# Four-layer conv_seq kernel: the token-major copy of layer 1's x made by vector-engine squares and DRAM transfers instead of TensorE transposes

## The chip, the core and the metric

The kernel is one program on one core of a Trainium2 chip, all arithmetic in float32. The metric is the device time of one execution in microseconds; the median of three runs before the change is 2450.09 us (2449.71 to 2451.28). The engines are TensorE (PE, with its weight loads shown apart as PEld), the vector engine (DVE), the scalar engine (ACT), GpSimd (POOL), and SyncE (SP), which issues every DMA of this kernel.

## The reference

x has four batches, 512 channels and 32x32 positions, that is 1024 tokens. Four layers follow each other:

- Layer 0: attention with 8 heads of 64 over the tokens, output projection, residual.
- Layer 1: linear attention, the subject of the change. With xf of shape (b, c, n):

```
Q = einsum('bcn,mc->bmn', xf, wq) + bq        # m = 64
K = einsum('bcn,mc->bmn', xf, wk) + bk
V = einsum('bcn,oc->bon', xf, wv) + bv
V = (max(xf, -1) + mean(xf, -1)) * V
Qf, Kf = softplus(Q)^T, softplus(K)
KV = einsum('bmn,bcn->bmc', Kf, V)
norm = 1 / einsum('bnm,bm->bn', Qf, sum(Kf, -1) + EPS)
x = x + gamma * einsum('bnm,bmc,bn->bcn', Qf, KV, norm)
```

- Layer 2: layer norm over the channels, attention with one head of 512, projection, residual.
- Layer 3: group norm, attention with 4 heads of 128, projection, residual.

## The kernel before

x of a batch lies in SBUF as 128 partitions x 4 chunks of channels x 1024 tokens; batches not in use go home to DRAM and come back. Most large products are made in seven half-size products instead of eight (`seven_products`, p1 to p7), whose sums and joins run on DVE (L774, L780, L739) and whose weight sums run on POOL (L695 to L698).

The kernel computes layer 1 without ever forming V: K^T x is formed first (`keys_times_x`, tokens on the contraction axis) and multiplied by wv afterwards (`keys_times_values`). For K^T x both the keys and x must have tokens on partitions. The function `linear_attention` returns seventeen pieces for one batch. They are: `gates` (the maximum over tokens on DVE, L1414, the sums on ACT, L1417); two `features` products of queries and keys, after which ACT adds a bias (L1407) and `softplus` runs over DVE and ACT (L1385 to L1391, with scratch tiles e, u and l); four `transpose_x`, each eight 128x128 transposes on TensorE (L1425) into PSUM and a copy of 128x1024 to a scratch tile, by ACT (L1432) or DVE (L1430) in turn; `transpose_keys` (L1438), which reads the block that the softplus wrote; `keys_times_x` (L1454), two calls to a piece; then the sum of keys, the division of queries, the transpose of K^T x, the product with wv (wv1, loaded at L599), and two `update` pieces.

Layer 1 of batch b-1 is woven into layer 0's projection of batch b: after every second product `slot()` emits one piece. This happens for batches 0, 1 and 2 (near 220, 460 and 700 us). Batch 3 has its pieces between the products of layer 2's start (950 to 1040 us), beside a layer norm. PE's program is in the order in which the code emits it; the other engines' programs are ordered by a scheduler, and every engine executes its program in order. So a piece that waits on PE holds everything behind it.

The scratch tiles are the v tiles of the batch being projected (batches 0 to 2) or a rotation of four tiles (batch 3). e is scratch 0, u scratch 1, l scratch 2; the ACT copies of `gates` go to scratch 3. x transposed, xt i, goes to scratch (i + 3) mod 4. The tile family "many" has one buffer; before the change it holds sums of probabilities in the attentions.

Lines that matter besides: L1084 and L1092 are layer 0's output projection of the same batch and its additions to x, L1051 the normalisation of the attention's output by quotients that come by DMA (L1033), L686 to L689 the four sums of a projection's inputs, L947 and L950 the sums of probabilities, L1492 a copy of the divided queries to the other 64 partitions.

## Time and profile before

| | |
|---|---|
| median of 3 runs | 2450.09 us (2449.71 to 2451.28) |
| profiled execution, its own time | 2450.76 us |
| its span, first to last instruction | 2449.0 us |
| PE busy | 2433.3 us |
| DVE busy | 1506.1 us |
| ACT busy | 704.6 us |
| POOL busy | 251.1 us |
| data moved by DMA | 88.64 MB, 36 GB/s on the mean |
| transposes of x on PE | 128, between 251.2 and 1003.2 us |

The time exceeds the span by 1.8 us, which lies around the program. The profile's times are counted from the start of the span. A line of a timeline gives start, duration, engine, source line, operation, output and inputs, shape and count, and in brackets the idle time of the engine ahead of it and what ended it. Durations of matmuls overlap, so PE's cost of a group is the distance to the next start. An "idle before" on PE itself would be time lost; on the other engines it is slack.

### The profile page before, as it was taken

The numbers are of one execution on the slowest core, as the hardware profiler recorded it, in microseconds if no ns is written. First come the engines' busy times: TensorE is split into PE (matmuls) and PEld (weight loads), VectorE is DVE, ScalarE is ACT, GpSimd is POOL, SyncE is SP. The second block draws the span as 40 slices with busy tenths as digits, with TensorE's granted clock in tenths as the row PEclk, the third lists the DMA queues.
The fourth block names the chain that finished last, engine by engine and source line by source line (L and its number), as shares of the span: only waits on it lengthen the run. The fifth ranks groups of instructions, "written<-read, shape, count | busy, mean of one in ns | idle before, by whom it ended". The sixth has DMA issues, their size and how long they took to land.

```text
span 2449.0 us, 24662 instructions
## 1 busy us (share of the span) xinstructions
PE 2433.3 (99%) x10098; PEld 1225.7 (50%) x10098; DVE 1506.1 (61%) x1798; ACT 704.6 (29%) x864; POOL 251.1 (10%) x240
## 2 busy tenths in 40 slices
PE   9999999999999999999999999999999999999999
PEld 4544544453455344644645446445556456555653
DVE  3677577757775788656595774763554554445344
ACT  1454144415531653221211201112321430332132
POOL 4001100110010001101103021021010001002000
PEclk9999999999999999999999999999999999999999
DMA  5000020002000301011001010110010001001001
GB/s 185 7 12 18 5 78 10 18 5 79 19 9 13 130 23 48 5 69 39 31 1 69 5 74 13 52 69 18 35 69 1 18 35 52 1 35 35 1 22 45
DMA packets 28959, 88.64 MB, mean 36 GB/s; under 512 B 2508, under 2 KB 10188, under 8 KB 25895
## 3 DMA queue, kind: packets, MB, share of 16 engines
q1 hardware_dynamic: 28838, 87.00, 9.9%
q8 instruction: 81, 1.33, 0.2%
q14 instruction: 40, 0.32, 0.0%
HBM read 60.59 MB, written 25.35 MB: 35 GB/s over the span
## 4 chain that ended last, share of the span: by engine, by line
PE 99%; DVE 1%; ACT 0%; issue 0%; DMA 0%; SPq 0%; DVEq 0%
PE acc L707 20%; PE acc L832 12%; PE acc L967 9%; PE acc L982 9%; PE sc L936 9%; PE sc L931 9%; PE acc L839 8%; PE acc L1084 7%; PE acc L1316 6%; PE acc L1277 2%; PE feat L641 1%; PE acc L1018 1%; PE acc L641 1%; PE upd L1520 1%; PE acc L1454 1%; PE xt L1425 1%
## 5 line engine op out<-in xcount | busy, mean ns | idle before, releaser
L941 ACT ACTIVATE pt<-sc 128x1024 f32<-128x1024 f32 x384 | 379.2, 1022 | 541.2 <-PE sc L936 304.0
L950 DVE TENSOR_TENSOR sum<-sum,pt 128x1024 f32<-128x1024 f32 x256 | 314.6, 1229 | 159.0 <-ACT pt L941 146.5
L967 PE MATMUL acc<-pt,v 64*64 64x512 f32 x2048 | 247.6, 591 | 0.0
L931 PE MATMUL sc<-q,k 64*64 64x512 f32 x2048 | 245.0, 591 | 1.1 <-ACT pt L941 1.1
L982 PE MATMUL acc<-pt,v 128*128 128x512 f32 x512 | 240.8, 594 | 0.0
L936 PE MATMUL sc<-q,k 128*128 128x512 f32 x512 | 239.9, 594 | 0.0
L707 PE MATMUL acc<-t,ws 128*128 128x512 f32 x384 | 173.9, 594 | 0.0
L695 POOL TENSOR_TENSOR ws<-wqkv 128x256 f32<-128x256 f32 (+1 forms) x40 | 39.7, 992 | 1307.1 <-PE acc L1018 523.2
L947 DVE TENSOR_TENSOR sum<-pt 128x1024 f32<-128x1024 f32 x64 | 78.0, 1219 | 137.4 <-ACT pt L941 137.4
L982 PEld LDWEIGHTS acc<-pt,v 128*128 128x128 f32 x512 | 96.8, 190 | 125.1 <-issue 121.4
L936 PEld LDWEIGHTS sc<-q,k 128*128 128x128 f32 x512 | 97.1, 191 | 115.9 <-issue 92.7
L967 PEld LDWEIGHTS acc<-pt,v 64*64 64x64 f32 x2048 | 78.3, 133 | 142.5 <-issue 140.3
L931 PEld LDWEIGHTS sc<-q,k 64*64 64x64 f32 x2048 | 77.3, 133 | 140.9 <-issue 131.9
L707 PEld LDWEIGHTS acc<-t,ws 128*128 128x128 f32 x384 | 72.6, 190 | 86.5 <-issue 85.0
L746 ACT COPY v<-acc 128x512 f32<-128x512 f32 x24 | 14.0, 585 | 308.6 <-PE acc L832 308.6
L678 DVE RECIPROCAL rd<-acc 128x512 f32<-128x512 f32 (+1 forms) x24 | 80.5, 3353 | 29.1 <-PE acc L1018 29.1
L832 PE MATMUL acc<-ws,t 128*128 128x256 f32 x384 | 87.3, 380 | 0.0
L839 PE MATMUL acc<-qs,w 128*128 128x512 f32 x192 | 86.6, 593 | 0.0
L839 PE MATMUL acc<-q,ln 128*128 128x512 f32 x192 | 85.8, 593 | 0.0
L1084 PE MATMUL acc<-ot,wo 128*128 128x256 f32 x336 | 80.7, 383 | 2.7 <-ACT ou L1103 2.7
L737 DVE TENSOR_TENSOR v<-acc,v 128x512 f32<-128x512 f32 x72 | 49.5, 689 | 51.5 <-PE acc L832 51.2
L746 ACT COPY q<-acc 128x512 f32<-128x512 f32 x40 | 23.4, 585 | 197.1 <-PE acc L707 197.1
(326 smaller groups left out, 3476.0 us busy)
## 6 DMA issues: line engine op xcount, KB each, us to landing
home<-x SPq DMA_DIRECT2D x8, 2048.0 KB
x<-home SPq DMA_DIRECT2D x8, 2048.0 KB
out<-x SPq DMA_DIRECT2D x32, 256.0 KB
rds<-quotients SPq DMA_DIRECT2D x30, 256.0 KB
rds<-quotients SPq DMA_DIRECT2D x7, 1024.0 KB
x<-in_x SPq DMA_DIRECT2D x3, 2048.0 KB
wo<-in_wo SPq DMA_DIRECT2D x3, 1024.0 KB
w<-in_w SPq DMA_DIRECT2D x1, 3072.0 KB
```

The source lines that it names most:

```text
L678: nc.vector.reciprocal(rd, ps)
L707: nc.tensor.matmul(ps, lhsT=w[:, m, :], rhs=x[:, m, :], start=start, stop=stop, skip_group_check=True)
L832: nc.tensor.matmul(ps[:, bass.ts(r, C // 2)], lhsT=x[:, m, bass.ts(2 * o + r, P)], rhs=w[:, m, :], start=(start and r == 0), stop=stop, sk ...
L839: nc.tensor.matmul(ps, lhsT=x[:, m, bass.ts(o, P)], rhs=w[:, m, :], start=start, stop=stop, skip_group_check=True,)
L931: nc.tensor.matmul(ps[half(h), s, :], lhsT=key(g, i)[half(s), half(h)], rhs=q[qb][half(s), g, :], start=True, stop=True,)
L936: nc.tensor.matmul(ps[:, s, :], lhsT=key(g, 2 * i + s), rhs=q[qb][:, g, :], start=True, stop=True)
L941: exps.append(nc.scalar.activation(pt, ps, AF.Exp, scale=scale).ins)
L950: adds.append(nc.vector.tensor_tensor(acc, acc, pt, ALU.add).ins)
L967: nc.tensor.matmul(outs[qb, g][r][half(s), :], lhsT=v[i // 2][half(r), i % 2, g * P + s * hd : g * P + (s + 1) * hd], rhs=pt[half(r), s, : ...
L982: nc.tensor.matmul(outs[qb, g][0], lhsT=v[j // 2][:, j % 2, bass.ts(g, P)], rhs=pt[:, s, :], start=(j == 0), stop=(j == NT - 1),)
L1084: nc.tensor.matmul(ps[i][:, bass.ts(o, n)], lhsT=w[:, m, bass.ts(o, P)], rhs=t[:, m, :], start=(start and m + o == 0), stop=(stop and m == ...
L1316: nc.tensor.matmul(ps[i, o], lhsT=w[m][:, bass.ts(o, P)], rhs=t[m], start=(start and m == 0), stop=(stop and m == 3), skip_group_check=True,)
```

## The change

The eight TensorE transposes and the PSUM copy of each `transpose_x` go. In their place DVE transposes x in squares of 32x32, in four instructions of 128x1024 to a batch, into a tile of the family "many". Each two of these (512 tokens) are then stored to a DRAM tile by four transfers of 256 KB, one for every 32 partitions, and read back by two transfers of 512 KB with tokens on partitions: twelve transfers to a batch. The channels come out in another order, so wv1's rows are loaded in that order too (four transfers in place of one), and `keys_times_x` streams its moving operand in runs of 32 elements. There are now two `transpose_x` pieces; `transpose_keys` follows them directly, in the place of the former third `transpose_x`, and two empty pieces keep `keys_times_x` at its slot.

```diff
-    nc.sync.dma_start(wv1, d["wv1"].rearrange("(c p) o -> p c o", p=P))
+    rows = d["wv1"].rearrange("(c a j) o -> c j a o", c=NC, a=NC)
+    for c in range(NC):
+        nc.sync.dma_start(wv1[c * SQUARE : (c + 1) * SQUARE], rows[c])
...
         def transpose_x(i):
-            ps = two_tile("xt")
-            for s in range(2):
-                for c in range(NC):
-                    nc.tensor.transpose(
-                        ps[:, s, bass.ts(c, P)], x[:, c, bass.ts(2 * i + s, P)], ident
-                    )
-            t["xt", i] = scratch((i + 3) % 4)
-            if i % 2:
-                nc.vector.tensor_copy(t["xt", i], ps)
-            else:
-                nc.scalar.copy(t["xt", i], ps)
+            squares = many_tile("squares").rearrange(
+                "p r (h n j) -> p r h n j", h=2, n=2 * NC
+            )
+            for h in range(2):
+                k = 2 * i + h
+                nc.vector.transpose(
+                    squares[:, :, h].rearrange("p r n j -> p n r j"),
+                    x[:, :, k * 2 * P : (k + 1) * 2 * P].rearrange(
+                        "p c (n j) -> p c n j", j=SQUARE
+                    ),
+                )
+            home = dram.tile([NC, NC, SQUARE, TB], F32, tag="squares", bufs=2, name="squares")
+            for a in range(NC):
+                nc.sync.dma_start(
+                    home[a].rearrange("r i f -> i r f"),
+                    squares[a * SQUARE : (a + 1) * SQUARE].rearrange("p r h n j -> p r (h n j)"),
+                )
+            for h in range(2):
+                xt = t["xt", 2 * i + h] = scratch((2 * i + h + 3) % 4)
+                nc.sync.dma_start(
+                    flat(xt).rearrange("p (a f) -> p a f", a=NC),
+                    home.rearrange("a r i (h f) -> h (r i) a f", h=2)[h],
+                )
...
-            xt = t.pop(("xt", i))
+            xt = flat(t.pop(("xt", i))).rearrange("p (b s j) -> p s b j", s=2, j=SQUARE)
...
-                    rhs=xt[:, s, :], start=(i == 0), stop=(i == NT // 2 - 1),
+                    rhs=xt[:, s], start=(i == 0), stop=(i == NT // 2 - 1),
...
             lambda: transpose_x(0),
             lambda: transpose_x(1),
-            lambda: transpose_x(2),
             transpose_keys,
-            lambda: transpose_x(3),
+            idle,
+            idle,
             both(lambda: keys_times_x(0), lambda: keys_times_x(1)),
```

In the changed program the scheduler places the four vector transposes of batches 0 to 2 so: the first after L686 and the second after L689 of the next projection's input sums, ahead of L1051; the third among the last L1092 additions; the fourth after the gate's first step (L1418). For batch 3 the first two stand between L950 sums near the end of layer 0's last attention, and the other two ahead of the reciprocal L1584 of layer 2's layer norm. Before the softplus's last step one more join (L739) stands than before. On SP, the first four stores and the first load follow the last quotients (L1033); for batch 3 the second four stores follow the load of wo.

## The prediction

> **What bounds the kernel now.** I read the engine shares and the chain of waits on the profile's page first.

> ```profile
> PE 2433.3 (99%) x10098; PEld 1225.7 (50%) x10098; DVE 1506.1 (61%) x1798; ACT 704.6 (29%) x864; POOL 251.1 (10%) x240
> PE 99%; DVE 1%; ACT 0%; issue 0%; DMA 0%; SPq 0%; DVEq 0%
> ```

> TensorE (PE) is the path from end to end: whatever leaves its program shortens the time, unless a wait takes its place. So the second view is the tile that goes, xt, with its durations in ns.

> ```profile
> L1425 PE MATMUL xt<-ident,x x128: 272/273/273, 251.2 to 1003.2; 128*128 128x128 f32 x128
> L1432 ACT COPY v<-xt x6: 992/1003/1015, 253.7 to 738.4; 128x1024 f32<-128x1024 f32 x6
> L1430 DVE COPY v<-xt x6: 1211/1218/1225, 259.1 to 747.0; 128x1024 f32<-128x1024 f32 x6
> ```

> 273 ns is a pipelined duration, not a price; the price is the distance between starts on PE's timeline (start, duration, instructions), here batch 0:

> ```profile
> 247.77 1.88 PE L707 MATMUL acc<-t,wqkv 128*128 128x512 f32 x4
> 249.49 1.88 PE L707 MATMUL acc<-t,ws 128*128 128x512 f32 x4
> 251.20 1.04 PE L1425 MATMUL xt<-ident,x 128*128 128x128 f32 x8
> 252.07 1.88 PE L707 MATMUL acc<-x,ws 128*128 128x512 f32 x4
> ...
> 260.02 1.04 PE L1425 MATMUL xt<-ident,x 128*128 128x128 f32 x8
> 260.89 3.60 PE L707 MATMUL acc<-t,ws 128*128 128x512 f32 x8
> 264.42 0.71 PE L1438 MATMUL keys<-ident,block 64*128 64x64 f32 x8
> ```

> Eight transposes take 252.07 - 251.20 = 0.87 us. The last row, the transpose of the keys (L1438), reads the block that the softplus finishes at L1391. So I read the vector engine (DVE) up to there, same columns:

> ```profile
> 253.83 1.22 DVE L1389 SCALAR_TENSOR_TENSOR v<-v,v 128x1024 f32<-128x1024 f32 x1 [1.08 <-ACT v L1388]
> 254.98 0.74 DVE L739 SCALAR_TENSOR_TENSOR q<-acc,cols,q 128x512 f32<-128x512 f32 x1
> 255.64 1.78 DVE L1390 TENSOR_TENSOR v<-v,v 128x1024 f32<-128x1024 f32 x1
> 257.34 0.74 DVE L739 SCALAR_TENSOR_TENSOR k<-acc,cols,k 128x512 f32<-128x512 f32 x1
> 258.00 1.21 DVE L1391 SCALAR_TENSOR_TENSOR block<-block,v 128x1024 f32<-128x1024 f32 x1
> ```

> The block is ready at 259.21, PE comes for it at 264.42: 5.2 us to spare. Batch 3, whose softplus has the sums of layer 2's normalised input ahead of it on DVE, has almost none: ready at 997.83, wanted at 998.26.

> ```profile
> 994.73 1.88 PE L707 MATMUL acc<-w,gq 128*128 128x512 f32 x4
> 996.45 1.88 PE L707 MATMUL acc<-w,ws 128*128 128x512 f32 x4
> 998.26 0.71 PE L1438 MATMUL keys<-ident,block 64*128 64x64 f32 x8
> ```

> ```profile
> 994.88 1.22 DVE L1430 COPY l<-xt 128x1024 f32<-128x1024 f32 x1
> 996.02 0.68 DVE L774 TENSOR_TENSOR q<-q,acc 128x512 f32<-128x512 f32 x1
> 996.61 1.22 DVE L1391 SCALAR_TENSOR_TENSOR block<-block,l 128x1024 f32<-128x1024 f32 x1
> ```

> **The change part by part** (line names of the kernel before). (1) PE loses 16 groups of eight transposes: 16 x 0.87 = -13.9 us. All of it is on the path.

> (2) The transpose of the keys moves up one piece: it takes the slot of the third transpose_x. It was reached after three groups of transposes (2.61 us) and one pair of products (260.89 to 264.42, 3.53 us) that are now gone or behind it, so PE arrives 6.14 us earlier, at 258.28. The softplus does not start earlier: it hangs on the second features product, ahead of every removed transpose. In the changed order of DVE one more L739 stands before the last softplus step: from 253.83 the steps are L1389 1.15, L739 0.66, L739 0.66, L1390 1.70, L739 0.66, L1391 1.21 (distances of the rows above), ready at 259.87. With 0.06 us for the signal (L1051's end at 939.58 to PE's start at 939.64) and 0.14 for the weight load that was hidden (L1438's LDWEIGHTS, 138 ns), PE goes on at 260.07. It gains 264.42 - 260.07 = 4.35 there, pays the pair afterwards (-3.53) and saves the fourth group (+0.87): 1.69 us per batch, three times, 5.1 us. The step L1390 is the uncertain one: 1.78 us in batches 0 to 2, where POOL works beside it, 1.22 in batch 3; with 1.22 the three batches give 1.7 us more.

> In batch 3 the only help is the missing L1430 (1.14 us by its step): the block is ready at 996.69, PE arrives at 998.26 - 6.14 = 992.12 and starts at 996.89. Gain 1.37, less 3.53, plus 0.87: -1.3 us. So this batch loses, behind a new gap of 4.8 us.

> The gap has a second possible price. After the idle 4.80 us at the program's start, L707's first instructions are issued 0.86 us apart until about 10 us (weight loads at 7.49, 8.35, 9.20) and 0.43 apart after it (10.98, 11.41): six times 0.43, 2.6 us lost. That bounds a slow restart at 0 and +2.6. I take 0, since at the start PE had not run at all before, and here it comes out of a millisecond of full work; the page's clock row can't decide, as it shows full speed at the start too.
> [...]

> (3) DVE gets 16 transposes of 128x1024 and loses eight copies (8 x 1.22). The trace has no such transpose. Bounds: 0.69 us (L1387, 128x1024 within SBUF) and 6.7 us (reciprocal, 3.35 us for 512); I take 1.22, the copy L1430, nearest in work. Cover: the first two of a batch stand among the four input sums (ending at 217.6) and before L1051; L1051 ends at 221.3 instead of 219.9, and PE reads it in the second L1084 group at 223.68. The tightest is batch 2: 694.93 + 2.44 + 1.29 = 698.7 against 701.00. Above some 2.4 us each this cover is gone, and L1084 waits. The third stands among the x updates, the fourth behind the gate's maximum; DVE idles from 245.29 to 249.12, so 2.4 us fit before the softplus. In batch 3 two stand among the sums of the last attention (DVE then idles 3.89 us before 933.31) and two in the idle 968.88 to 972.42, 3.5 us. Price 0.
> [...]

> (4) DMA: per batch eight stores of 256 KB and four loads of 512 KB on SP's queue. Rows: 2 MB of x went home in 6.64 us (issue 316.91, its buffer reused at 323.55); 512 KB of quotients took 5.0 us (213.62 to 218.61). So 1 MB of stores takes 3.3 to 10 us, and the first four, issued from about 220, land by 232 with their issues (some 0.5 us each). The third transpose needs that, as the squares have one buffer, and comes at 233.9; what queues behind its wait on DVE are two x updates, the gate and the joins, with the 3.8 us of idle less 2.4. The last load needs softplus's l, free at 259.87; three loads at 5 us each end by 270 to 275, while keys_times_x wants the first two at 271.3 and the others at 276.7. Behind them SP has only the copy of queries at 295.81 and the home transfer at 316.91; in batch 3, the stores that wait for DVE stand before the v loads (916.06) with some 4 us to spare and behind wo (948.52). Price 0. The three extra wv1 loads are issued near 14 us, used at 297: 0.

> (5) keys_times_x streams x in 128-byte runs. Its eight groups of 1.85 us are bounded by 0 and a doubling, +14.8. I take 0: L1084, whose moving operand is cut from wider rows, costs per column what L707 costs (1.73 us for eight of 256, 3.44 for eight of 512). ACT loses eight copies of 1.0 us off the path: 0.

> Sum: 5.1 - 1.3 = 3.8 us less than the profiled execution's 2450.76: 2447.0. That execution stood 0.67 above the median 2450.09, so 2446.3, 0.15% faster: the 13.9 us become a wait for the softplus.

> **The rivals.** (a) The softplus wait is smaller: L1390 runs in 1.22 and the weight load hides: 3.8 + 1.7 + 0.6 = 6.1 us, 2444.0. For it: batch 3's row of 1.22. Against it: POOL's sums start 0.9 us earlier too and still overlap. With no wait at all it would be 2436.2; the order of DVE excludes that nearly. (b) The gap of batch 3 costs the slow restart, +2.6: 2448.9. (c) Slower: the vector transposes are slow. From 2.4 us each L1084 waits twice the excess in each of three batches, and batch 3 pays from 1.8 on, again twice: eight times the excess in all. At 4 us it is some 10 to 15 us on top, 2456 to 2461; at 6.7 about +35, 2481. It decides for slower than 0.2% (+8.7 on my sum) from about 3.4 us. The reciprocal's row speaks for such rates, the copies against. (d) The DMAs are late: stores landing after 237, or loads after 276; each us late is 3 to 4 us in all, 2455 and more from 3 us late. The quotients' rate speaks against it. (e) The strided stream doubles keys_times_x: 2461.

> **How the numbers follow.** About 0.2% (4.9 us) is what a measurement of this kernel tells from no change. As worked 0.48 (from 2444.5 to 2448.5, of it 0.10 under 2445.2), (a) 0.16, (b) 0.14, (c) 0.09, (d) 0.08, (e) 0.05. Faster 0.26, within 0.2% 0.52, slower 0.22. The likeliest case gives 2446.3; the range takes in (a), (b) and the milder half of (c) and (d): 2443 to 2458.

> **What would show it.** PE: no xt; keys waiting on the block for about 1.8 us in batches 0 to 2 and 4.8 us in batch 3, on PE's timeline near 258 and 980 to 990; after the latter, instruction distances of 0.43 (or 0.86, case b). DVE: transposes of about 1.2 us and none waiting for a DMA. No wait of keys_times_x on a DMA, its groups still 1.87 us. The sum is wrong if L1084 waits for ot, if the softplus starts late, or if the third transpose waits for the squares' stores.

## The result and the profile after

The changed kernel takes 2448.55 us (median of 12 executions, 2446.95 to 2449.81) against 2450.32 us (12 executions, 2449.71 to 2451.94) for the kernel before in the same comparison. The ratio is 0.9991, with a 95% interval of 0.9984 to 0.9999. Of the 13.9 us that TensorE (PE) no longer spends on transposes, 1.8 us arrive in the time. The profiled execution took 2449.3 us, its span 2447.6 us.

In what follows the lines have the names of the changed kernel: up to the softplus they are four higher than before (L1391 became L1395, L1390 became L1394, L1051 became L1055, L707 became L711), behind it 22 higher (the keys' transpose L1438 became L1460, `keys_times_x` L1454 became L1476). The stream transposes are L1437, the stores L1445, the loads L1451.

Engine shares, and the chain that ended last:

```profile
PE 2423.6 (99%) x9970; PEld 1209.2 (49%) x9970; DVE 1510.2 (62%) x1806; ACT 697.4 (28%) x856; POOL 250.9 (10%) x240
PE 96%; DVE 2%; ACT 1%; issue 1%; DMA 0%; SPq 0%; DVEq 0%
```

PE is busy 9.7 us less, not 13.9, so some of its remaining work became slower; and the share of the vector engine (DVE) in the chain has gone from 1% to 2%. PE's waits (who waits, for whom; us in total, times, longest us):

```profile
PE keys L1460 <- DVE block L1395: 7.0, 4, 4.4
PE acc L711 <- DMA wqkv<-in_wqkv: 4.5, 1, 4.5
PE acc L1088 <- ACT ou L1107: 2.7, 4, 0.7
...
PE acc L1003 <- DVE ot L982: 0.6, 1, 0.6
PE acc L711 <- DVE w L691: 0.2, 1, 0.2
```

The first row is new, as are the last two; the second is the program's start, and the third stands with the same 2.7 us in the kernel before. The first row is one wait per batch. Batch 0 on PE's timeline (start, duration, instructions, idle before and its releaser):

```profile
254.48 1.88 PE L711 MATMUL acc<-t,wqkv 128*128 128x512 f32 x4
256.37 1.96 PE L711 MATMUL acc<-x,ws 128*128 128x512 f32 x4
259.20 0.71 PE L1460 MATMUL keys<-ident,block 64*128 64x64 f32 x8 [0.88 <-DVE block L1395]
259.84 7.13 PE L711 MATMUL acc<-t,ws 128*128 128x512 f32 x16
...
270.34 1.94 PE L1476 MATMUL acc<-v,kf 128*64 128x512 f32 x8
```

PE comes for the keys at 258.3 and stands 0.88 us. `keys_times_x` starts at 270.34 where it started at 273.00; 0.16 us of that was there already at 254, from the program's start, so the batch gained 2.50 us. Such a comparison of the same product's start in two kernels is called PE's order below. The same holds for batches 1 and 2: by 750 us the changed kernel is 7.65 us ahead.

Batch 3 loses. First the place of the long wait:

```profile
979.12 7.11 PE L711 MATMUL acc<-w,ws 128*128 128x512 f32 x16 [0.23 <-DVE w L691]
990.60 1.12 PE L1460 MATMUL keys<-ident,block 64*128 64x64 f32 x8 [4.38 <-DVE block L1395]
991.65 3.78 PE L711 MATMUL acc<-w,gq 128*128 128x512 f32 x4
995.22 2.61 PE L711 MATMUL acc<-w,ws 128*128 128x512 f32 x4
997.67 1.88 PE L711 MATMUL acc<-ln,ws 128*128 128x512 f32 x4
```

PE stops at 986.2 and goes on at 990.60. Then four products whose like takes 1.88 us take 3.78, and the next four 2.61. The clock row in windows of one us (window, length, PE busy, granted clock, busy share of the DMA engines, GB/s) says why:

```profile
988.00:989.00 1.00, 0.00 (x0) 1.00 0.61 121
989.00:990.00 1.00, 0.00 (x0) 0.93 1.08 383
990.00:991.00 1.00, 0.40 (x4) 0.50 0.58 148
...
995.00:996.00 1.00, 1.00 (x2) 0.50 0.00 0
996.00:997.00 1.00, 1.00 (x3) 0.66 0.00 0
997.00:998.00 1.00, 1.00 (x3) 1.00 0.00 0
```

The granted clock is half from 989.86 (0.93 is 0.86 us at full and 0.14 at half) to 996.68, 6.8 us; PE resumes 0.74 us after it begins. All twelve executions have a mean granted clock of 0.998, like the profiled one, where the kernel before has 1.000 in its profile. The keys' transposes cost 0.42 us more, the two pairs 1.75 and 0.73: 2.9 us on top of the wait. From 750 us to the end of batch 3 the lead shrinks from 7.65 to 2.2 us: 1.1 us go in the last attention of layer 0 (below), 0.4 at L691, 1.0 in the wait net of what the batch saved, 2.9 in the slow clock.

The new operations themselves, from the view of the tile `squares` (durations in ns: lowest, median, highest):

```profile
L1437 DVE STREAM_TRANSPOSE squares<-x x16: 1235/1238/1246, 213.8 to 963.3; 128x1024 f32<-128x1024 f32 x16
```

and from the DMA issues (KB each, median us from issue to landing):

```profile
squares<-squares SPq DMA_DIRECT2D x32, 256.0 KB, 4.3
v<-squares SPq DMA_DIRECT2D x12, 512.0 KB, 4.6
```

No entry among the waits of PE or DVE names a store or a load of the squares, and L1476 keeps 1.87 us for eight products with its moving operand in 128-byte runs.

### The profile page after: what moved, and what is told of

Its sections match the earlier page's. It is cut to its first block, busy times and chain, and to the rows that moved or that the text cites. A ratio compares the mean times of both kernels' runs of the same rounds, so it can differ in the third digit from the quotient of the medians.

```text
span 2447.6 us, 24505 instructions
## 1 busy us (share of the span) xinstructions
PE 2423.6 (99%) x9970; PEld 1209.2 (49%) x9970; DVE 1510.2 (62%) x1806; ACT 697.4 (28%) x856; POOL 250.9 (10%) x240
## 4 chain that ended last, share of the span: by engine, by line
PE 96%; DVE 2%; ACT 1%; issue 1%; DMA 0%; SPq 0%; DVEq 0%
PE acc L711 18%; PE acc L836 12%; PE acc L971 9%; PE acc L986 9%; PE sc L940 9%; PE sc L935 9%; PE acc L843 8%; PE acc L1088 7%; PE acc L1320 6%; PE acc L1281 2%; PE feat L645 1%; PE acc L1022 1%; PE acc L645 1%; PE upd L1542 1%; PE acc L1476 1%; PE kv L645 1%
## 5 line engine op out<-in xcount | busy, mean ns | idle before, releaser
L711 PE MATMUL acc<-t,ws 128*128 128x512 f32 x384 | 173.4, 593 | 0.0
L711 PEld LDWEIGHTS acc<-t,ws 128*128 128x128 f32 x384 | 72.7, 190 | 88.0 <-issue 87.5
L1088 PE MATMUL acc<-ot,wo 128*128 128x256 f32 x336 | 80.6, 383 | 2.7 <-ACT ou L1107 2.7
```

What stands on the lines that cost most here:

```text
L711: nc.tensor.matmul(ps, lhsT=w[:, m, :], rhs=x[:, m, :], start=start, stop=stop, skip_group_check=True)
L1088: nc.tensor.matmul(ps[i][:, bass.ts(o, n)], lhsT=w[:, m, bass.ts(o, P)], rhs=t[:, m, :], start=(start and m + o == 0), stop=(stop and m == ...
```

## The experiments

Theory: the gain is lost because the keys' transpose now stands ahead of its softplus on PE; the wait costs time by itself, and in batch 3 also by the half clock that follows it. Rival 1: the place of the keys is harmless, and the squares, their transfers or the strided stream take the time. Rival 2: the slow products near 990 to 997 come from the transfers that run at that moment (up to 383 GB/s), not from the gap. The edits are to the changed kernel's list of pieces or to `transpose_keys` if not said otherwise; all of these kernels compute every output.

**Keys one or two pieces later.** The first kernel swaps the keys with one empty piece, the second with both:

```
             lambda: transpose_x(0),
             lambda: transpose_x(1),
-            transpose_keys,
             idle,
+            transpose_keys,        # first kernel
             idle,
+            transpose_keys,        # second kernel, instead
```

> transpose_keys one slot later than in the changed kernel, all else the same. Theory (the lost gain is PE's wait for the softplus, and in batch 3 a slow restart after the 4.4 us gap): batches 0 to 2 wait no more (3 x 0.98 us back), batch 3 waits about 0.9 us and stays at full rate (6.4 us back): 2448.5 - 9.3 = 2439.2 us. Rival 1 (the squares and their transfers cost the rest by contention on DVE or DMA): at most 1 or 2 us back, 2447. Rival 2 (the slow matmuls of batch 3 come from the loads of x that land at the same time, not from the gap): 2442.

> transpose_keys two slots later, right before keys_times_x. Theory: no wait on the softplus in any batch; against the changed kernel 3 x 0.98 us in batches 0 to 2 and 7.8 us in batch 3 come back: 2448.5 - 10.7 = 2437.8 us, all of the 13.9 us but about 1.1. Rival 1 (contention): 2447 or so. Rival 2 (loads slow the matmuls of batch 3): 2441.

Measured: 2439.69 us (2438.66 to 2440.86), ratio 0.9959 (0.9945 to 0.9972), with one later; 2439.66 us (2438.63 to 2439.84), ratio 0.9957 (0.9943 to 0.9970), with two. Both are faster than both kernels, by 10.4 us against before. With one later, batch 3's keys do not wait either, where I had expected 0.9 us. PE's waits with two later, without the program's start and rows that the kernel before has too:

```profile
PE acc L711 <- DVE q L784: 1.2, 1, 1.2
...
PE acc L1003 <- DVE ot L982: 0.6, 1, 0.6
PE acc L711 <- DVE w L691: 0.2, 1, 0.2
```

and batch 3 on its PE timeline:

```profile
983.85 1.99 PE L711 MATMUL acc<-w,gq 128*128 128x512 f32 x4 [1.16 <-DVE q L784]
985.67 1.88 PE L711 MATMUL acc<-w,ws 128*128 128x512 f32 x4
```

The wait on the softplus is gone in all four batches, and the granted clock is 1.00 from 985 to 1000, with the loads of the squares moving 274 GB/s between 985 and 990. A small wait stands in its place: the next products need a join on DVE (L784) that lies behind a softplus step. It explains most of the 1.9 us by which the second kernel came out above its expectation. The sum closes on PE's order: the last products come 11.5 us earlier than before, of which 0.8 were there at 200 us already, from the program's start, so 10.7 are the change's. Batches 0 to 2 gain 3.45 us each, batch 3 only 1.9, 1.6 less than its four groups of transposes, most of it the wait for L784; L1003 (below) takes 1.1 and L691 0.4: 13.9 - 1.6 - 1.1 - 0.4 = 10.8. The strided stream, the stores and the loads therefore take nothing that shows.

**Only batch 3's keys later.**

```
-            transpose_keys,
-            idle,
-            idle,
+            *([idle, idle, transpose_keys] if b == B - 1
+              else [transpose_keys, idle, idle]),
```

> Only batch 3 has transpose_keys two slots later; batches 0 to 2 are as in the changed kernel. Theory: 7.8 us back, of them 3.0 from the restart, 2440.7 us. Rival 2 (matmuls slowed by the loads): 4.8 us back, 2443.7. Rival 1: 2448.

Measured: 2442.69 us (2442.06 to 2443.28), ratio 0.9971 (0.9959 to 0.9982). Batch 3 alone is worth 5.9 us of the 8.9 that both together bring; the remaining three waits of 0.9 us cost 0.95 each on PE's order (a gain of 2.50 instead of 3.45), 2.9 of the other 3.0. The miss of 2 us against the expectation has a place: PE waits 1.5 us for L784, which I had not counted.

**The gap filled with work that nobody reads.** Ahead of batch 3's keys PE gets products of ones with x:

```
-            ps = two_tile("keys")[:, 0, :]
+            both_halves = two_tile("keys")
+            ps = both_halves[:, 0, :]
+            for c in range(NC if b == B - 1 else 0):     # NC is 4
+                nc.tensor.matmul(both_halves[:, 1, :], lhsT=ones,
+                                 rhs=x[:, c, :TB], start=True, stop=True)
```

> The changed kernel with four products of 128x512 that nobody reads, put before batch 3's transpose_keys, so that PE works through 3.4 us of its 4.4 us gap. Theory (the gap causes the slow restart): the wait shrinks to about 1 us, the matmuls after it keep 0.43 us distance and PE's clock row stays at 1.00, 3.0 us back: 2445.5 us although PE has 3.4 us more work. Rival 2 (loads slow them): the matmuls stay slow, 2448.5 us. Rival 1: 2448.5 us or more.

Measured: 2445.51 us (2444.51 to 2446.34), ratio 0.9982 (0.9973 to 0.9991). Its PE timeline:

```profile
984.82 3.60 PE L1461 MATMUL keys<-x,ones 128*128 128x512 f32 x8
989.37 0.71 PE L1465 MATMUL keys<-ident,block 64*128 64x64 f32 x8 [0.95 <-DVE block L1395]
990.00 1.99 PE L711 MATMUL acc<-w,gq 128*128 128x512 f32 x4
```

PE does 3.4 us more work than in the changed kernel and the kernel is 3.0 us faster. The keys wait for the same softplus; only the idle time ahead of them is 0.95 us instead of 4.38, the products behind them take 1.99 us instead of 3.78, and the clock stays at 1.00. The wait itself and the slow clock behind it are two separate prices, and the second is 3.0 us (2.8 if each kernel is taken against the kernel before of its own comparison).

**The kernel before with early keys.** The transposes stay on PE; only the keys move up, by one piece:

```
             lambda: transpose_x(1),
-            lambda: transpose_x(2),
             transpose_keys,
+            lambda: transpose_x(2),
             lambda: transpose_x(3),
```

> The kernel before with transpose_keys one slot earlier, as the change places it; x is still transposed on PE. Theory (the place of the keys' transpose costs, not the way of x): batches 0 to 2 lose 0 to 0.2 us (PE arrives at 260.0, the block is ready at 259.2 to 259.9), batch 3 waits about 4 us and may restart slowly (+3): 2454.5 to 2457.5 us. Rival 1 (the squares' contention took the gain): no change, 2450.3 us.

Measured: 2457.07 us (2455.70 to 2458.53) against 2450.70, ratio 1.0027 (1.0016 to 1.0037). Its timeline and its clock windows behind the gap:

```profile
997.92 0.68 PE L1438 MATMUL keys<-ident,block 64*128 64x64 f32 x8 [3.96 <-DVE block L1391]
998.53 3.21 PE L707 MATMUL acc<-w,gq 128*128 128x512 f32 x4
```

```profile
998.00:999.00 1.00, 1.00 (x9) 1.00 0.00 0
999.00:1000.00 1.00, 1.00 (x3) 0.57 0.00 0
1000.00:1001.00 1.00, 1.00 (x3) 0.50 0.00 0
...
1002.00:1003.00 1.00, 1.00 (x3) 0.72 0.00 0
```

There is not one stream transpose in this kernel, and moving one piece costs 6.4 us. In the profiled execution 5.7 us of it are batch 3's on PE's order; 0.5 went in the last attention of layer 0, where DVE also waited longer for the quotients (1.12 us against 0.63). The slow products come with no byte moved (the last two columns are 0), while two pieces later the changed kernel had 274 GB/s and full speed. That ends rival 2, and rival 1 as an explanation of the loss.

**Both ways at once.** The changed kernel's path is used, and PE also makes the 32 transposes of 128x128 per batch in the slots of the kernel before, unread and without the copies out of PSUM; the keys stand in the old slot:

```
+        def unread(i):
+            ps = two_tile("xt")
+            for s in range(2):
+                for c in range(NC):
+                    nc.tensor.transpose(ps[:, s, bass.ts(c, P)],
+                                        x[:, c, bass.ts(2 * i + s, P)], ident)
...
-            lambda: transpose_x(0),
-            lambda: transpose_x(1),
+            both(lambda: unread(0), lambda: transpose_x(0)),
+            both(lambda: unread(1), lambda: transpose_x(1)),
+            lambda: unread(2),
             transpose_keys,
-            idle,
-            idle,
+            lambda: unread(3),
```

> PE's program as in the kernel before, with x's transposes on PE that nobody reads, and x taken from the squares and their twelve transfers. The vector transposes and the transfers are thus added and only the PSUM copies are gone. Theory: they are covered but for about 1.1 us near batch 3's first two squares: 2450.3 to 2451.5 us. Rival 1 (contention): 3 us or more above the kernel before, 2453.5 and up.

Measured: 2451.95 us (2451.27 to 2452.76) against 2450.70, ratio 1.0005 (0.9996 to 1.0014). That is 0.45 us above the expected range, and the interval takes in no difference. On PE's order the profiled execution loses 1.2 us between 200 us and the end. So 16 stream transposes, 32 stores, 16 loads and the strided stream together, less the copies out of PSUM, cost about 1.2 us. One wait is new against the kernel before, and it is the 0.6 us at L1003, PE's product with ones in layer 0's last attention. The changed kernel shows where that comes from, on PE and on DVE (one fence each):

```profile
905.89 1.02 PE L1003 MATMUL acc<-sum,ones 64*64 64x512 f32 x2
907.52 0.65 PE L1003 MATMUL acc<-sum,ones 64*64 64x512 f32 x3 [0.61 <-DVE ot L982]
...
917.98 7.13 PE L645 MATMUL g<-w 128*128 128x512 f32 x16
```

```profile
898.60 1.24 DVE L1437 STREAM_TRANSPOSE squares<-x 128x1024 f32<-128x1024 f32 x1
...
900.86 1.24 DVE L1437 STREAM_TRANSPOSE squares<-x 128x1024 f32<-128x1024 f32 x1
902.02 2.51 DVE L954 TENSOR_TENSOR sum<-sum,pt 128x1024 f32<-128x1024 f32 x2
...
906.79 0.68 DVE L982 TENSOR_TENSOR ot<-ot,acc 128x512 f32<-128x512 f32 x1
```

Both of batch 3's first two stream transposes stand among the sums of probabilities without an idle stretch until L982, which PE wants at 906.9. From L1003 to the product g PE takes 12.09 us (905.89 to 917.98) where it took 10.94 before (913.55 to 924.49), so the place loses 1.1 us, more than the idle time that is listed; in the kernel with both ways it is 1.1 as well. That leaves 0.1 of the 1.2 us for all the rest.

**How long a gap must be.** Two last kernels are the one with unread products, with one and with two products in place of four (`range(1 ...)`, `range(2 ...)`).

> Like the run with four unread products ahead of batch 3's keys, with one product only (0.86 us of TensorE work, all outputs computed): TensorE then stands for about 3.5 us instead of 4.4 before batch 3's keys. The wait itself ends at the same moment in each case, so only the clock can make a difference. [...]

> With two unread products (1.72 us of TensorE work, all outputs computed): TensorE stands for about 2.7 us before batch 3's keys. Full clock after the gap and 2445.5 us, as with four products, if a gap under 3 us is harmless; 2448.5 us with the half clock after it if every gap of some us brings it.

Measured: 2448.27 us (2446.80 to 2449.43) with one product, 2445.95 us (2445.62 to 2446.84) with two. In the profiled executions the gaps were 3.52 and 2.66 us, and both show a half clock. The windows with one product:

```profile
990.00:991.00 1.00, 1.00 (x5) 1.00 0.81 279
991.00:992.00 1.00, 1.00 (x3) 0.60 0.85 286
...
994.00:995.00 1.00, 1.00 (x3) 0.69 0.00 0
```

and with two:

```profile
989.00:990.00 1.00, 0.54 (x8) 1.00 0.91 254
990.00:991.00 1.00, 1.00 (x5) 0.79 0.84 290
...
993.00:994.00 1.00, 1.00 (x2) 0.50 0.09 30
994.00:995.00 1.00, 1.00 (x4) 1.00 0.00 0
```

By these fractions the half clock runs from 991.20 to 994.62 and from 990.58 to 994.00: 3.42 us in each, and each costs 1.70 us on PE's order. The expectation that a gap under 3 us is harmless fails in the second of these executions: 2.66 us of idle time were enough. It does not fail in every execution: the profiled one with two products (2446.84 us) is the slowest of its eight, and the fastest (2445.62) lies at the level of the kernel with four products (2445.51), which a stretch that costs 1.7 us would not leave it. The three fastest (2445.62 to 2445.73) also have a mean granted clock of 1.000 against 0.999 in the profiled one; a single stretch takes 0.0007 off the mean and would not leave 1.000. With one product the profiled execution (2446.80 us) is the fastest of eight; that the six above 2447.9 have two stretches fits their times and their mean granted clock (0.998, against 0.999 in the profiled one), but no trace of them shows it.

## Why the prediction was right, and by which steps it was not

The predicted 2446.3 us stood 2.2 us below the measured 2448.55, within the stated range, and the case "within 0.2%", which had the highest chance, is what came. Measured against before in the same comparison, 1.8 us were gained where 3.8 were forecast.

- **Step 1, 13.9 us off PE's path: right but for 0.4.** With the keys two pieces later 10.4 us arrive in the time, and nearly all of the missing ones have a wait. One of these waits the step overlooked: the input sum w that L691 makes was ready 0.64 us before PE came for it (985.47 against 986.11 in the kernel before), and PE now comes 0.87 us sooner, one group of transposes; it loses 0.4 us there.
- **Step 2, the keys' transpose would wait for the softplus: right in place and kind.** PE came for the block at 258.3 as worked out, and batch 3's gap was 4.38 us against 4.8; the batch lost 1.0 us by it instead of 1.3.
- **Step 2, the duration of L1390: wrong size.** I took 1.78 us because POOL's weight sums would still run beside it. They do, but L1394 took 1.22. The two rows of the changed kernel, DVE and then POOL:

```profile
256.14 1.22 DVE L1394 TENSOR_TENSOR v<-v,v 128x1024 f32<-128x1024 f32 x1
```

```profile
256.25 1.68 POOL L702 TENSOR_TENSOR ws<-wqkv,ws 128x256 f32<-128x256 f32 x1
```

  In the kernel before POOL was first:

```profile
255.60 0.74 POOL L697 TENSOR_TENSOR ws<-wqkv 128x256 f32<-128x256 f32 x1
256.30 1.71 POOL L696 TENSOR_TENSOR ws<-ws,wqkv 128x256 f32<-128x256 f32 x1
```

  There DVE's step began at 255.64, 0.04 us after POOL's L697, and took 0.56 us longer than alone; here POOL's began 0.11 us after DVE's and took 0.95 us longer than its 0.73, to 0.57 us past the end of DVE's. In both orders the step that starts second is the slow one, and batches 1 and 2 show the same durations (1.77 and 1.78 us for L1390, 1.22 twice for L1394). My argument that "POOL still overlaps" was true and still gave the wrong duration, since it did not ask who would be first. The weight load of 0.14 us was not exposed either: the products follow the keys' start by 0.64 us as elsewhere. The gain was 2.50 us a batch instead of 1.69, 2.4 us over three batches: rival (a) was right on this term.
- **Step 2, the slow restart priced 0: wrong.** Rival (b) had it, with a price of 2.6 us; it measured 2.9 in the trace and 2.8 to 3.0 by the filled gap. My reason, that PE comes out of a millisecond of full work, carries no weight: 4 us without work were enough (3.96 in the kernel before with early keys), and with two unread products 2.66. The half clock lasted 3.42 us with one and with two unread products and in the kernel before with early keys (999.14 to 1002.56), and 6.82 us, twice that, in the changed kernel. Which gaps bring one stretch, which two and which none is not shown.
- **Step 3, the stream transposes at 1.22 us and price 0: right on the duration, wrong on one cover.** They took 1.24 us, so rival (c) never came near. Third and fourth transposes did not move the softplus, and no L1088 waits for ot longer than before. The cover that failed is one I had called given, two transposes "among the sums of the last attention": DVE's idle 3.89 us lay behind the place where PE needs L982. It costs 1.1 us.
- **Steps 4 and 5, the transfers and the strided stream at 0: right.** Stores landed 4.3 us after issue and loads 4.6; with PE's work unchanged all of it cost 1.2 us, 1.1 of them at L1003. Rivals (d) and (e) fall.

Added up in PE's order: 3 x 2.50 = 7.5, less 1.0 and 2.9 in batch 3, less 1.1 at L1003, less 0.4 at L691, makes 2.1 us (the 2.2 above holds the 0.16 from the start). Against the 3.8 of the prediction lie wrong terms of +2.4, +0.3, -2.9, -1.1 and -0.4 in it; that the sum came within 2 us is in good part luck, their cancelling.

## What to carry to other kernels

Work taken off the engine that bounds the kernel also brings forward what stands behind it: where that reads another engine's result, move it back. Here that is one line of the list of pieces, one piece later was enough, and it turned 1.8 us into 10.4. The gap of 4.38 us on TensorE had two prices here, the idle time and the half clock behind it (2.8 to 3.0 us), and work that nobody reads was cheaper than the gap (2445.51 us against 2448.55); moving useful work into it was better than both (2439.69 us).
